# A four-layer image kernel on one Trainium2 core: the closing block of the last image, its loads, its setup and its first product are put in another order

## The chip, the cores and the metric

The kernel runs on one core of a Trainium2 chip. What is measured is the time of one execution on the device, in microseconds (us). A core has five engines that each work through their own instructions in order: PE (TensorE, matrix products; PEld is its weight load), DVE (VectorE), ACT (ScalarE), POOL (GpSimd) and SP (SyncE, which here issues the DMA transfers). They wait for each other by semaphores. PE writes only to PSUM, of which there are eight banks.

## The reference, cut to what matters

Four layers work on four images of 64 x 64 pixels with 128 channels. Layer 0 and layer 1 contain state scans over the image. The change lies where layer 1 ends for the last image and layer 2 begins. Layer 1 closes with

```python
y = ym[:, 0] + ...                         # sum of the four scan directions, 256 channels
y = _ln(y, onorm_w, onorm_b)               # over the channels
y = y * _silu(z)
x = input + y @ out_proj_w                 # 256 -> 128 channels
h2 = _ln(x, ln2_w, ln2_b)
h2 = gelu(h2 @ fc1_w + fc1_b) @ fc2_w + fc2_b   # 128 -> 512 -> 128
return x + h2
```

and layer 2 begins with `norm = _ln(tokens, ln1_w, ln1_b)` of its first image; each pixel is then joined with its nine neighbours in two small networks (`d_w1`, `r_w1`: "drive" and "resistance") that gate a weighted mean. Layer 2 needs all of the first image before it can begin, but the first image was finished by layer 1 long before the last one.

## The kernel before, in words

An image is held as 128 channels by 4,096 pixels and cut into eight chunks of 512 pixels (`NCH` = 8, `T` = 512); a chunk of 128 channels is 256 KB. The scans of both layers come first (until about 11,020 us). The last scan's result, `yd`, is 256 channels: two halves `i` = 0, 1. For every image but the last, layer 1's closing block runs as side work between the scans. For the last image nothing is left to run beside, and class `Last` does it at the beginning of `layer2`. Everything there is in the order in which it is written (`manual_schedule`), on each engine.

`layer2` first builds `Edges` (`E`). Its constructor loads the weights `w`, `rel`, `v` (L1471 to L1477) and does the setup: small products on PE with additions on DVE (`wcen`, `wnei`, `relb`, `inb`, `w2`), `obc`, `mass`, `gsp` (with one Exp and one Ln on ACT), four memsets of `near` on POOL (L1549) and two copies into `vals` on DVE (L1551).

Then `last.early()` issues the loads of the weights `wts`, and of `x` and `z` for all chunks (L1356, L1358); `z` is the gate of layer 1, already through silu. `statistics(0, range(NCH))` is layer 2's first normalization of image 0, chunk by chunk in four steps: load `xs` (L1568, two buffers), center it by a product and copy it to `norm` with ACT (L1572, L1573), square it on POOL (L1577), and form the variance by a product that ACT copies to `rstd` (L1586, L1587). `last.late()` issues the loads of `y` (L1363). `E.roots([E.rstd])` makes reciprocal roots of all the variances by two ACT instructions over 4,096 columns (L1761, L1763).

`in_turn` then runs the generators `last.first(c)`, one per chunk: in each turn one more chunk begins, and all running chunks do one stage, the oldest first. A stage ends at `yield`. The stages of `first` are:

1. product with `neg256` into bank `out0` (one buffer), L1378: minus the mean over 256 channels
2. additions to `y` on DVE (L1382, twice), squares into `tmp` on ACT (L1383) and POOL (L1384)
3. product with `ones128` into `out1` (L1388), then `over_root`: Ln and Exp on ACT into `rs`, which has two buffers (L1367, L1368)
4. scaling by `rs`, shift, and multiplication by `z`: four scalar-tensor-tensor instructions on DVE (L1393, L1394)
5. product with the output projection into a bank `mm` (two buffers) and the residual addition on DVE (L1398, L1399)
6. centering product into `cen` (L1402), square on ACT (L1404), copy on DVE (L1405)
7. variance product into `mm` (L1408) and `over_root`
8. multiplication by `rs` on DVE (L1411)

Each product of float32 is two passes of 512 columns for each half of the channels. After all chunks have gone through `first`, `second` does the two fully connected layers with Gelu (L1423, L1424, L1428, L1429) and stores, again in turn; two pieces of `project(0, range(4))` (scale `norm` by `rstd` on POOL, L1596, then products with `wnei`, L1600) go into each of its turns. The two banks `mm` are shared by the setup, the statistics, `first`, `second` and `project`.

Of the kernel before, what the change touches and what calls it, by code (L numbers as in the profile page):

```python
# [9 lines left out]
F32 = mybir.dt.float32  # L10
# [7 lines left out]
P = 128  # L18
# [3 lines left out]
T = 512  # L22
NCH = L // T
# [17 lines left out]
def chunk(c):  # L41
    return slice(c * T, (c + 1) * T)
# [185 lines left out]
class ScanWeights:  # L228
# [27 lines left out]
    def load(self):  # L256

        nct, most = self.nct, max(TILES)
        tile = self.pool.tile([P, most * ND * (H + P)], F32, name="xpdt", tag="xpdt", bufs=1)
        self.xp = tile[:, 0 : nct * ND * H].rearrange("p (t k h) -> p t k h", t=nct, k=ND)  # L260
        at = most * ND * H
        self.dtw = tile[:, at : at + ND * nct * P].rearrange("p (k c) -> p k c", k=ND)
        self.nc.sync.dma_start(out=self.xp, in_=self.d_xp)
        for i in range(HALVES):
            self.nc.sync.dma_start(out=self.dtw[i * H : (i + 1) * H], in_=self.d_dtw)
# [1068 lines left out]
class Last:  # L1334
# [14 lines left out]
            return self.psum.tile([P, 2, T], F32, name="cen", tag="cen", bufs=2)  # L1349
        return self.psum.tile([P, T], F32, name=tag, tag=tag, bufs=2 if tag == "mm" else 1)  # L1350

    def early(self):
        self.wt = self.tile("wts", 1, (P, 1280))
        self.nc.sync.dma_start(out=self.wt, in_=self.side.w1b)
        for c in range(NCH):
            self.nc.sync.dma_start(out=self.x[c], in_=self.side.x1[self.b, :, chunk(c)])  # L1356
            for i in range(2):
                self.nc.sync.dma_start(out=self.z[c][:, i, :], in_=self.side.szd[1, self.b, i][:, chunk(c)])  # L1358

    def late(self):  # L1360
        for c in range(NCH):
            for i in range(2):
                self.nc.sync.dma_start(out=self.y[c][:, i, :], in_=self.side.yd[1, self.b, i][:, chunk(c)])  # L1363

    def over_root(self, ps, scale):
        rs = self.tile("rs")
# [4 lines left out]
    def first(self, c):  # L1371

        nc, C, side = self.nc, self.C, self.side
        x, y, z = self.x[c], self.y[c], self.z[c]
        outp = self.wt[:, 0:256].rearrange("p (t c) -> p t c", t=2)
        ps = self.bank("out0")
        for i in range(2):
            nc.tensor.matmul(ps, C.neg256, y[:, i, :], start=i == 0, stop=i == 1)  # L1378
        yield
        sq = self.tile("tmp", 2, (P, 2, T))  # L1380
        for i in range(2):
            nc.vector.tensor_add(y[:, i, :], y[:, i, :], ps)  # L1382
        nc.scalar.activation(sq[:, 0, :], y[:, 0, :], AF.Square)  # L1383
        nc.gpsimd.tensor_mul(sq[:, 1, :], y[:, 1, :], y[:, 1, :])  # L1384
        yield
        ps = self.bank("out1")
        for i in range(2):
            nc.tensor.matmul(ps, C.ones128, sq[:, i, :], start=i == 0, stop=i == 1)  # L1388
        rs = self.over_root(ps, 0.5)
        yield  # L1390
        for i in range(2):
            n, w, b = y[:, i, :], side.onw[:, i : i + 1], side.onb[:, i : i + 1]
            nc.vector.scalar_tensor_tensor(n, n, w, rs, ALU.mult, ALU.mult)  # L1393
            nc.vector.scalar_tensor_tensor(n, n, b, z[:, i, :], ALU.add, ALU.mult)  # L1394
        yield
        ps = self.bank("mm")
        for i in range(2):
            nc.tensor.matmul(ps, outp[:, i, :], y[:, i, :], start=i == 0, stop=i == 1)  # L1398
        nc.vector.tensor_add(x, x, ps)  # L1399
        yield  # L1400
        ps = self.bank("cen")[:, 0, :]
        nc.tensor.matmul(ps, C.cen128, x, start=True, stop=True)  # L1402
        sq = self.tile("tmp", 2, (P, 2, T))[:, 0, :]
        nc.scalar.activation(sq, ps, AF.Square)  # L1404
        nc.vector.tensor_copy(y[:, 0, :], ps)  # L1405
        yield
        ps = self.bank("mm")
        nc.tensor.matmul(ps, C.ones128, sq, start=True, stop=True)  # L1408
        rs = self.over_root(ps, 1.0)
        yield  # L1410
        nc.vector.tensor_mul(y[:, 0, :], y[:, 0, :], rs)  # L1411
# [21 lines left out]
def in_turn(stages):  # L1433


    waiting, running = list(stages), []
    while waiting or running:
        running += waiting[:1]
        waiting = waiting[1:]
        running = [stage for stage in running if next(stage, stage) is None]  # L1440
        yield


NB = 9
# [7 lines left out]
class Edges:  # L1452
# [8 lines left out]

    def __init__(self, tc, C, es, nb, x_in, x_out, d_w, d_rel, d_v):
        self.nc, self.C, self.x_in, self.x_out = tc.nc, C, x_in, x_out
        nc = self.nc
        wp = es.enter_context(tc.tile_pool(name="l2w", bufs=1))
        self.pool = self.ahead = None
        self.psum = es.enter_context(tc.tile_pool(name="l2p", bufs=1, space=PSUM))
        self.dram = es.enter_context(tc.tile_pool(name="l2d", bufs=1, space=DRAM))

        w = wp.tile([P, d_w.shape[1]], F32, name="w")  # L1470
        nc.sync.dma_start(out=w, in_=d_w)  # L1471
        w1 = w[:, 0:768].rearrange("p (m t c) -> p m t c", m=2, t=3)
        self.vw, self.ow = w[:, 768:896], w[:, 896:1024]
        rel = wp.tile([8, 2 * P + NB], F32, name="rel")
        nc.sync.dma_start(out=rel, in_=d_rel)
        v = wp.tile([P, d_v.shape[1]], F32, name="v")
        nc.sync.dma_start(out=v, in_=d_v)  # L1477
        ln1w, ln1b, self.ln2w, self.ln2b, vb, ob = (v[:, i : i + 1] for i in range(6))
        b1, w2 = v[:, 6:8], v[:, 8:10]
        self.db2, self.rb2, gamma, self.lam, self.ebias = (v[:, i : i + 1] for i in range(10, 15))  # L1480
# [11 lines left out]
        for m in range(2):  # L1492
            ps = self.bank()
            nc.tensor.matmul(ps[:, 0:NB], rel[:, m * P : (m + 1) * P], rel[:, 2 * P :], start=True, stop=True)
            nc.vector.tensor_scalar_add(self.relb[:, m, :], ps[:, 0:NB], b1[:, m : m + 1])
            ps = self.bank()
            nc.tensor.matmul(ps[:, 0:1], self.wcen[:, m, :], ln1b, start=True, stop=True)
            nc.vector.tensor_scalar_add(self.relb[:, m, :], self.relb[:, m, :], ps[:, 0:1])
            ps = self.bank()
            nc.tensor.matmul(ps[:, 0:1], self.wnei[:, m, :], ln1b, start=True, stop=True)  # L1500
            nc.vector.tensor_copy(self.inb[:, m : m + 1], ps[:, 0:1])
            for t in range(NB):
                nc.vector.tensor_copy(self.w2[:, m, t, t : t + 1], w2[:, m : m + 1])
        ps = self.bank()
        nc.tensor.matmul(ps[:, 0:1], self.vw, ln1b, start=True, stop=True)
        nc.vector.tensor_add(self.inb[:, 2:3], ps[:, 0:1], vb)
        for m in range(2):
            nc.vector.tensor_scalar_mul(self.wcen[:, m, :], self.wcen[:, m, :], ln1w)
            nc.vector.tensor_scalar_mul(self.wnei[:, m, :], self.wnei[:, m, :], ln1w)
        nc.vector.tensor_scalar_mul(self.vw, self.vw, ln1w)  # L1510

        mean = wp.tile([P, 1], F32, name="mean")
        nc.vector.reduce_sum(mean, self.ow, axis=AX.X)
# [3 lines left out]
        nc.tensor.matmul(ps[:, 0:1], C.cen128, ob, start=True, stop=True)  # L1517
        self.obc = wp.tile([P, 1], F32, name="obc")
        nc.vector.tensor_copy(self.obc, ps[:, 0:1])


        fold = wp.tile([P, 32], F32, name="fold")
# [7 lines left out]
        for j in range(4):  # L1530
            part = slice(32 * j, 32 * j + 32)
            nc.vector.tensor_copy(self.mass[part, part], row[part].to_broadcast([32, 32]))

        self.gsp = wp.tile([P, 1], F32, name="gsp")
        zero = wp.tile([P, 1], F32, name="zero")
# [3 lines left out]
        nc.scalar.activation(self.gsp, self.gsp, AF.Ln, bias=1.0)  # L1539
        nc.vector.scalar_tensor_tensor(self.gsp, gamma, zero, self.gsp, ALU.add, ALU.max)  # L1540
        nc.vector.tensor_scalar_add(self.gsp, self.gsp, 1e-6)

# [2 lines left out]
        for tiles in self.near:  # L1547
            for t in tiles:
                nc.gpsimd.memset(t, 0.0)  # L1549
        for t in self.vals:  # L1550
            nc.vector.tensor_copy(t.rearrange("p h w -> p (h w)"), vb.to_broadcast([P, HR * PW]))  # L1551
        self.norm = [wp.tile([P, NCH, T], F32, name=f"norm{i}") for i in range(min(nb, 2))]
        self.rstd = wp.tile([P, NCH, T], F32, name="rstd")

    def bank(self):
        return self.psum.tile([P, T], F32, name="mm", tag="mm", bufs=2)
# [314 lines left out]
def layer2(tc, C, nb, x_in, x_out, d_w, d_rel, d_v, beside, side):  # L1871
    with ExitStack() as es, tc.manual_schedule():
        E = Edges(tc, C, es, nb, x_in, x_out, d_w, d_rel, d_v)

        def run(pieces):
            for piece in pieces:
                piece()

        def statistics(b, chunks):
            return staggered([E.statistics(b, c) for c in chunks]) if b < nb else []  # L1880
# [4 lines left out]
        if True:  # L1885
            with tc.tile_pool(name="last", bufs=1) as pool:
                E.pool = pool
                last = Last(tc, C, pool, E.psum, side, nb - 1, x_in)
                last.early()
                run(statistics(0, range(NCH)))  # L1890
                last.late()
                E.roots([E.rstd])
                for _ in in_turn([last.first(c) for c in range(NCH)]):
                    pass
                pieces = project(0, range(4))
                for _ in in_turn([last.second(c) for c in range(NCH)]):
                    for _ in range(2):
                        if pieces:
                            pieces.pop(0)()
                run(pieces)  # L1900
# [3 lines left out]
            out, halves, rest = None, [], []  # L1904
            for b in range(nb):
                for s in range(2):
                    if s == 0:
                        early = project(b, [4]) + [E.edge_row]
                        ahead = merged(project(b, range(5, 8)), statistics(b + 1, range(5)))
                        second = E.rstd[:, 5:8, :]  # L1910
                    else:
                        early = []
# [18 lines left out]
                    out = E.edges(b, s, at, sides, following)  # L1931
# [3 lines left out]
            pieces = E.finish(*third)  # L1935
# [519 lines left out]
```

## Time and profile before

| | us |
|---|---|
| median of 3 runs | 12947.81 (12925.22 to 12954.68) |
| the profiled execution's own time | 12949.75 |
| its span | 12948.0 |
| busy DVE / POOL / PE / ACT over the span | 11775.1 / 9661.8 / 9408.4 / 7767.4 |
| last scan output stored, first load of `w` issued | 11021.8 |
| first product of `Last.first` (L1378) | 11066.4 |
| first Gelu of `Last.second` (L1424) | 11164.0 |

The durations and instants below come from the one profiled execution. In a line of the timeline the columns are: start, time, engine, line of the code, operation, output<-input with their shapes, count, and in brackets the idle time before it and what ended that. In the chain of waits each line is a start, a duration and the work that ended last there. In the table of stretches each engine has its busy time and, in parentheses, its count of instructions; PEclk is the granted clock of TensorE as a share of full speed, and the last two columns are the busy share of the DMA engines and GB/s.

### The profile page before, as it was taken

To read this page: it belongs to the slowest core of one execution; us is meant where nothing else is said; L and a number is where in the kernel's file an instruction comes from. 1 tells how busy PE (TensorE), PEld (TensorE's weight loads), DVE (VectorE), ACT (ScalarE), POOL (GpSimd) and SP (SyncE) were. 2 spreads that over 40 slices of the span, in tenths; PEclk is the share of its full clock that TensorE was granted. 3 is DMA by queue.
4 is the path that set the end of the run, shared out by engine and by line. 5 is a ranking of instruction groups with operands and counts; after the bars stand their busy time and mean duration, and the time that the engine had idled before them with its cause. 6 is when DMAs were issued, how large, how long until landed. Compare 5 with 4: busy or idle time off the path is not lost.

```text
span 12948.0 us, 128061 instructions
## 1 busy us (share of the span) xinstructions
PE 9408.4 (73%) x40881; PEld 2751.0 (21%) x41435; DVE 11775.1 (91%) x7219; ACT 7767.4 (60%) x10392; POOL 9661.8 (75%) x3167
## 2 busy tenths in 40 slices
PE   6777777777767677677776677776777777775799
PEld 1111111111111111111111121111112121221455
DVE  8999999999999889999999999999999999498566
ACT  4666656655666546655666555555555554476576
POOL 6887888887878778887888788888888888166200
PEclk8888899889989888998889899989898888887899
DMA  6888888898888878898878987777877876255200
GB/s 180 212 223 230 218 224 218 216 227 221 211 221 210 214 199 207 220 229 213 210 219 209 227 209 200 205 200 198 218 196 200 204 197 172 66 145 132 70 21 17
DMA packets 873449, 2463.66 MB, mean 190 GB/s; under 512 B 141887, under 2 KB 163527, under 8 KB 865095
## 3 DMA queue, kind: packets, MB, share of 16 engines
q1 hardware_dynamic: 872775, 2455.44, 74.1%
q8 instruction: 330, 5.41, 0.2%
q14 instruction: 344, 2.82, 0.1%
HBM read 2035.79 MB, written 268.17 MB: 178 GB/s over the span
## 4 chain that ended last, share of the span: by engine, by line
DVE 36%; issue 18%; PE 15%; DMA 14%; POOL 8%; ACT 7%; SPq 1%; DVEq 0%; another core or an unknown queue 0%; POOLq 0%; ACTq 0%
DVE h L478 19%; DVE h L459 13%; DMA h<-dud 8%; POOL h L459 4%; PE ms L102 3%; PE da L467 2%; POOL delta L102 2%; DMA pad<-xid 1%; PE yps L559 1%; ACT s L2128 1%; ACT da L469 1%; DMA repC<-xdd 1%; DVE s L2115 1%; PE B L504 1%; POOL low L102 1%
## 5 line engine op out<-in xcount | busy, mean ns | idle before, releaser
L459 POOL TENSOR_TENSOR h<-h,repC 128x2048 f32<-128x2048 f32 x1536 | 6952.0, 4531 | 1489.0 <-ACT state L496 1194.2
L478 DVE TENSOR_TENSOR_SCAN h<-da,state,h 128x1024 f32<-128x1024 f32 x2304 | 5293.4, 2337 | 278.8 <-ACT da L469 164.9
L469 ACT ACTIVATE da<-da,av 128x1024 f32<-128x1024 f32 x3072 | 3327.6, 1087 | 2914.9 <-PE da L467 2481.5
L467 PE MATMUL da<-dp,spread 128*128 128x512 bf16 x5802 | 2002.3, 425 | 2406.7 <-DVE h L478 2368.4
L459 DVE TENSOR_TENSOR h<-h,B 128x2048 f32<-128x2048 f32 x1536 | 3474.9, 2262 | 194.1 <-issue 91.4
L559 PE MATMUL yps<-h,gather 128*32 128x512 f32 x12288 | 1876.5, 687 | 19.4 <-issue 4.8
L478 DVE TENSOR_TENSOR_SCAN h<-da,h 128x1024 f32<-128x1024 f32 x768 | 1719.4, 2278 | 68.3 <-ACT da L469 29.2
L467 PEld LDWEIGHTS <-spread 128*128 128x128 bf16 x6144 | 589.7, 102 | 4480.6 <-issue 4086.9
L565 PE MATMUL yps<-ones,nothing 128*128 128x512 bf16 x4197 | 1237.9, 405 | 38.0 <-issue 34.4
L102 ACT ACT_TABLE_LOAD x580 | 744.1, 1283 | 12.2 <-DMA x<-in_x_dram 2.2
L102 ACT CAST parts<-delta 128x1024 bf16<-128x1024 f32 x384 | 400.6, 1043 | 548.4 <-POOL delta L102 521.4
L102 POOL TENSOR_TENSOR delta<-delta,low 128x1024 f32<-128x1024 f32 x192 | 452.3, 2356 | 264.2 <-ACT low L102 213.5
L565 PEld LDWEIGHTS <-nothing 128*128 128x128 bf16 x4409 | 383.0, 101 | 1226.3 <-issue 934.1
L2159 POOL COPY wide_total<-total 128x128 f32<-128x128 f32 x128 | 37.4, 293 | 781.1 <-DVE total L2157 214.4
L102 PE MATMUL ms<-d,wts 128*128 128x512 f32 (+3 forms) x832 | 486.8, 697 | 170.4 <-POOL d L102 67.0
L102 PE MATMUL ms<-xd,xpdt 64*128 64x512 f32 x768 | 484.6, 714 | 108.6 <-ACT delta L102 26.2
L102 POOL TENSOR_TENSOR low<-delta,xc 128x1024 f32<-128x1024 f32 x192 | 502.5, 2617 | 9.1
L2128 ACT ACTIVATE s<-s,least 128x512 f32<-128x512 f32 x512 | 368.4, 720 | 231.3 <-DVE least L2115 227.7
L542 PE MATMUL yps<-y,ident 128*128 128x512 f32 x576 | 499.2, 956 | 4.6 <-issue 1.5
L1792 POOL TENSOR_TENSOR acc<-acc,part 128x1024 f32<-128x1024 f32 x120 | 301.9, 2519 | 198.4 <-DVE part L1786 198.4
L102 ACT ACTIVATE low<-ms,av 128x512 f32<-128x512 f32 x384 | 263.7, 687 | 291.1 <-PE ms L102 266.9
L102 POOL TENSOR_TENSOR parts<-delta,parts 128x1024 bf16<-128x1024 f32 x192 | 409.2, 2132 | 29.7 <-ACT parts L102 18.4
(295 smaller groups left out, 11070.9 us busy)
## 6 DMA issues: line engine op xcount, KB each, us to landing
h<-dud SPq DMA_DIRECT2D x3072, 512.0 KB
dp<-parts SPq DMA_DIRECT2D x2304, 64.0 KB
repC<-xdd SPq DMA_DIRECT2D x192, 512.0 KB
dud<-low SPq DMA_DIRECT2D x192, 512.0 KB
spread<-gd SPq DMA_DIRECT2D x72, 1024.0 KB
pad<-xid SPq DMA_DIRECT2D x176, 256.0 KB
x<-x SPq DMA_DIRECT2D x104, 256.0 KB
yd<-y SPq DMA_DIRECT2D x96, 256.0 KB
```

Of the source, the lines that this page charges most:

```text
L102: return call(*args, **kw)
L459: engine.tensor_mul(pair, pair, t.prepared[step][name].unsqueeze(1).to_broadcast([P, 2, TS]))
L467: self.nc.tensor.matmul(da[:, cols], self.C.spread[:, jj, :], dp[:, j, cols], start=True, stop=True)
L469: self.nc.scalar.activation(da, da, AF.Exp, scale=t.W.a[:, at : at + 1])
L478: nc.vector.tensor_tensor_scan(h[:, way], da[:, way], h[:, way], 0.0 if step % NSTEP == 0 else t.states[step - 1][:, u % NG : u % NG + 1], ...
L504: self.nc.tensor.matmul(rep[:, self.half(i)], t.W.pick[at, :], t.prepared[step]["xd"][at, :], start=True, stop=True)
L542: self.nc.tensor.matmul(self.like_part(yps, k), self.C.ident, self.part(t.y, k, c, b), start=True, stop=False)
L559: self.nc.tensor.matmul(out, self.C.gather[jj], rhs, start=False, stop=jj == 3)
L565: self.nc.tensor.matmul(self.live["yps"], self.C.nothing, self.C.ones16, start=False, stop=False, skip_group_check=True)
L1792: (nc.vector if alone and pair else nc.gpsimd).tensor_add(acc, acc, part)
L2115: self.nc.vector.tensor_tensor_reduce(out=self.live["s", n][:, h, :], in0=self.live["sps", n][:, h, :], in1=self.bias[case][:, h, :], scal ...
L2128: self.nc.scalar.activation(s, s, AF.Exp, scale=-1.0, bias=self.live["least", n][:, h : h + 1], accum_out=self.live["total", n][:, h : h + 1],
```

## The change

The loads of `Last` are issued chunk by chunk, `y` first, then `z`, then `x`; `wts` follows chunk 0's `z`, and the three weight loads of `Edges` follow chunk 0. The setup of `Edges` becomes a generator of twelve pieces and a rest; these pieces, the 32 pieces of the first statistics and one piece for the roots are put into the turns of `first`, four in each from the second turn on, behind the stages of that turn. With that the setup lies in turns 1 to 3 (turns counted from 0), the first two `xs` loads in turn 4, the other statistics in turns 5 to 12 and the roots in turn 12. Of `first`, stages 1 and 2 are one stage, so a chunk takes seven stages and the block fourteen turns for fifteen.

```diff
-    def early(self):
-        self.wt = self.tile("wts", 1, (P, 1280))
-        self.nc.sync.dma_start(out=self.wt, in_=self.side.w1b)
-        for c in range(NCH):
-            self.nc.sync.dma_start(out=self.x[c], in_=self.side.x1[self.b, :, chunk(c)])
-            for i in range(2):
-                self.nc.sync.dma_start(out=self.z[c][:, i, :], in_=self.side.szd[1, self.b, i][:, chunk(c)])
-
-    def late(self):
-        for c in range(NCH):
-            for i in range(2):
-                self.nc.sync.dma_start(out=self.y[c][:, i, :], in_=self.side.yd[1, self.b, i][:, chunk(c)])
+    def load(self, c):
+        nc, side, b, cols = self.nc, self.side, self.b, chunk(c)
+        for i in range(2):
+            nc.sync.dma_start(out=self.y[c][:, i, :], in_=side.yd[1, b, i][:, cols])
+        for i in range(2):
+            nc.sync.dma_start(out=self.z[c][:, i, :], in_=side.szd[1, b, i][:, cols])
+        if c == 0:
+            self.wt = self.tile("wts", 1, (P, 1280))
+            nc.sync.dma_start(out=self.wt, in_=side.w1b)
+        nc.sync.dma_start(out=self.x[c], in_=side.x1[b, :, cols])
...
             nc.tensor.matmul(ps, C.neg256, y[:, i, :], start=i == 0, stop=i == 1)
-        yield
         sq = self.tile("tmp", 2, (P, 2, T))
...
+    def load(self):
+        for to, source in zip((self.w, self.rel, self.v), self.sources):
+            self.nc.sync.dma_start(out=to, in_=source)
+
+    def setup(self):
...
             for t in range(NB):
                 nc.vector.tensor_copy(self.w2[:, m, t, t : t + 1], w2[:, m : m + 1])
+            yield
...
         for tiles in self.near:
             for t in tiles:
                 nc.gpsimd.memset(t, 0.0)
+                yield
         for t in self.vals:
             nc.vector.tensor_copy(t.rearrange("p h w -> p (h w)"), vb.to_broadcast([P, HR * PW]))
+            yield
...
-                last.early()
-                run(statistics(0, range(NCH)))
-                last.late()
-                E.roots([E.rstd])
-                for _ in in_turn([last.first(c) for c in range(NCH)]):
-                    pass
+                last.load(0)
+                E.load()
+                for c in range(1, NCH):
+                    last.load(c)
+                setup = E.setup()
+                pieces = [lambda: next(setup, None)] * 14 + statistics(0, range(NCH))
+                pieces.append(lambda: E.roots([E.rstd]))
+                for turn, _ in enumerate(in_turn([last.first(c) for c in range(NCH)])):
+                    for _ in range(4 if turn else 0):
+                        if pieces:
+                            pieces.pop(0)()
+                run(pieces)
```

The other additions of `yield` in `setup` end the pieces for `m` = 0 and 1, for `inb` with the scaling of the weights by `ln1w`, for `obc`, for `mass` and for `gsp`. The tiles `norm` and `rstd` are made in the constructor.

More of the change, by code (lines that the diff above doesn't have):

```diff
@@ L1463, in __init__ @@
         self.nc, self.C, self.x_in, self.x_out = tc.nc, C, x_in, x_out
-        nc = self.nc
         wp = es.enter_context(tc.tile_pool(name="l2w", bufs=1))
@@ L1468, in __init__ @@
         self.dram = es.enter_context(tc.tile_pool(name="l2d", bufs=1, space=DRAM))
-        w = wp.tile([P, d_w.shape[1]], F32, name="w")
-        nc.sync.dma_start(out=w, in_=d_w)
+        self.wp, self.sources = wp, (d_w, d_rel, d_v)
+        self.w = wp.tile([P, d_w.shape[1]], F32, name="w")
+        self.rel = wp.tile([8, 2 * P + NB], F32, name="rel")
+        self.v = wp.tile([P, d_v.shape[1]], F32, name="v")
+        self.norm = [wp.tile([P, NCH, T], F32, name=f"norm{i}") for i in range(min(nb, 2))]
+        self.rstd = wp.tile([P, NCH, T], F32, name="rstd")
+    def load(self):
+        for to, source in zip((self.w, self.rel, self.v), self.sources):
+            self.nc.sync.dma_start(out=to, in_=source)
+    def setup(self):
+        nc, wp, C, w, rel, v = self.nc, self.wp, self.C, self.w, self.rel, self.v
         w1 = w[:, 0:768].rearrange("p (m t c) -> p m t c", m=2, t=3)
         self.vw, self.ow = w[:, 768:896], w[:, 896:1024]
[L1474 to L1477, printed above, removed]
         ln1w, ln1b, self.ln2w, self.ln2b, vb, ob = (v[:, i : i + 1] for i in range(6))
@@ L1532, in __init__ @@
             nc.vector.tensor_copy(self.mass[part, part], row[part].to_broadcast([32, 32]))
+        yield
         self.gsp = wp.tile([P, 1], F32, name="gsp")
@@ L1541, in __init__ @@
         nc.vector.tensor_scalar_add(self.gsp, self.gsp, 1e-6)
+        yield
         self.near = [[wp.tile([P, HR, PW], F32, name=f"near{m}{s}") for s in range(2)] for m in range(2)]
@@ L1549, in __init__ @@
                 nc.gpsimd.memset(t, 0.0)
+                yield
         for t in self.vals:
             nc.vector.tensor_copy(t.rearrange("p h w -> p (h w)"), vb.to_broadcast([P, HR * PW]))
-        self.norm = [wp.tile([P, NCH, T], F32, name=f"norm{i}") for i in range(min(nb, 2))]
-        self.rstd = wp.tile([P, NCH, T], F32, name="rstd")
+            yield
     def bank(self):
@@ L1888, in layer2 @@
                 last = Last(tc, C, pool, E.psum, side, nb - 1, x_in)
-                last.early()
-                run(statistics(0, range(NCH)))
-                last.late()
-                E.roots([E.rstd])
-                for _ in in_turn([last.first(c) for c in range(NCH)]):
-                    pass
+                last.load(0)
[10 more added lines that the diff above has]
+                run(pieces)
+                assert next(setup, setup) is setup
                 pieces = project(0, range(4))
```

## The prediction

> **What bounds the kernel now.** Whole-page shares say nothing here: the change lies in one stretch of some 220 us near 11,020 us. All times below in two or three digits are microseconds after 11,000 of the trace (25.9 is 11025.9). I read the busy time by stretch first, cut at the steps of the code: loads and setup, first statistics, first chunk until the two large ACT instructions end, the pipelined turns of `first`, their drain, `second`.
>
> ```profile
> core 0: us, PE busy (x) PEld busy (x) DVE busy (x) ACT busy (x) POOL busy (x), PEclk, DMA share, GB/s
> 11021.80:11041.50 19.70, 4.19 (x16) 3.90 (x16) 10.24 (x53) 0.41 (x2) 7.72 (x4) 0.50 0.95 322
> 11041.50:11066.00 24.50, 16.85 (x32) 5.67 (x33) 0.00 (x0) 8.78 (x15) 8.31 (x8) 0.81 0.60 193
> 11066.00:11074.60 8.60, 4.28 (x10) 1.43 (x8) 2.57 (x4) 7.92 (x4) 2.08 (x2) 1.00 0.84 315
> 11074.60:11136.60 62.00, 47.84 (x91) 19.83 (x92) 30.35 (x45) 18.56 (x30) 5.77 (x5) 0.86 0.00 0
> 11136.60:11164.00 27.40, 19.32 (x32) 6.04 (x30) 19.12 (x24) 12.46 (x20) 12.14 (x8) 0.81 0.00 0
> ```
>
> Until 66.0 no chunk of the closing block has begun. Row one is transfers (95% DMA), row two a chain of statistics in which DVE does nothing. Then the chain of waits shows who ends last:
>
> ```profile
> 11036.14 5.36 DMA z<-szd
> 11041.51 5.33 DMA xs<-x
> ...
> 11067.23 3.72 ACT rstd L1761
> 11070.97 3.62 ACT rstd L1763
> 11075.16 3.80 PE out L1388 x4
> ```
>
> The xs loads sit in SP's order behind 24 loads of x and z, the y loads behind xs, and the roots (7.36 us) hold ACT while chunk 0 waits for its square. Third, the timeline of one full turn:
>
> ```profile
> 11122.82 0.69 DVE L1399 TENSOR_TENSOR x<-x,mm 128x512 f32<-128x512 f32 x1
> 11126.32 1.28 DVE L1382 TENSOR_TENSOR y<-y,out 128x512 f32<-128x512 f32 x2
> 11127.65 1.98 PE L1378 MATMUL out<-y,neg 128*128 128x512 f32 x4 [3.16 <-DVE y L1382]
> 11131.19 1.88 PE L1398 MATMUL mm<-y,wts 128*128 128x512 f32 x4
> 11133.11 0.69 DVE L1399 TENSOR_TENSOR x<-x,mm 128x512 f32<-128x512 f32 x1
> 11137.81 0.68 DVE L1411 TENSOR_TENSOR y<-y,rs 128x512 f32<-128x512 f32 x1
> 11138.58 0.69 ACT L1367 ACTIVATE rs<-mm,eps 128x512 f32<-128x512 f32 x1 [0.57 <-DVE y L1411]
> 11139.35 10.85 POOL L1596 TENSOR_TENSOR norm<-norm,rstd 128x512 f32<-128x512 f32 x7
> 11140.45 0.69 DVE L1405 COPY y<-cen 128x512 f32<-128x512 f32 x1 [1.96 <-ACT tmp L1404]
> 11141.06 0.68 DVE L1399 TENSOR_TENSOR x<-x,mm 128x512 f32<-128x512 f32 x1
> 11142.43 1.63 DVE L1394 SCALAR_TENSOR_TENSOR y<-y,v,z 128x512 f32<-128x512 f32 x1
> ```
>
> PE's first product waits 3.16 us in each turn for the additions of the chunk before (bank out0 has one buffer): a loop of 10.29 us, 122.82 to 133.11. The next turn has no such product and takes 7.95.
>
> **The change, part by part.** *Loads.* Byte count and order change, the rate does not. The first 512 KB issued at 21.79 are w today, and their waiter starts at 25.93; they become y of chunk 0, so its product can start at 25.9 instead of 66.4. Ahead of y of chunk 1 and with it lie 2.94 MB; today 1.8 MB have moved by 30.0 (222 GB/s) and 378 GB/s follow, so it lands at 33. A chunk is then 1.31 MB, 3.5 us; all 11.7 MB are in by 57. From turn 2 on no y is late. The xs loads follow; they are first used near 68, so they are hidden.
>
> *Turns 0 to 4 (fill).* Each DVE sum takes this trace's durations: additions 1.28, four scalar-tensor-tensors 2.9, residual addition 0.6, copy 0.69; POOL square 1.04.
> Turn 0: product with the clock at 0.50, 3.5 (as for the product at 115.89, 3.46), then 1.28, 1.04: 31.8.
> Turn 1: ones product of chunk 0 to 33.7, product of chunk 1 to 35.6, additions to 36.9. Then setup pieces 1 to 4, 25.93 to 32.22 today, 5.8 here: 42.7. They stand ahead of chunk 0's scaling on DVE: exposed.
> Turn 2: scaling 45.6, additions 46.9, setup pieces 5 and 6 (3.3 today) 50.2; POOL squares until 48.1, then two memsets (1.98 each) until 52.
> Turn 3: residual 50.8, scaling 53.7, additions 55.0, the two vals copies (2.56) 57.6; POOL squares to 56.2, two memsets to 60.1.
> Turn 4: copy, residual 58.9, scaling 61.7, additions 63.0.
> So the setup's 11.7 us of DVE is paid nearly in full, though transfers would have filled some of it.
>
> *Full turns.* The product no longer waits for the additions of its own turn, because the bank was freed a turn earlier: 3.16 us off. What is next late? PE's own sum, 16 passes at 0.43, is 6.9. But the two `rs` buffers tie ACT to DVE: residual +2.8 (second L1393) frees `rs`; Ln, Exp 1.4; Square 0.65; the Ln of the older chunk 0.69, Exp 0.63, Square 0.6; copy 0.7: 8.0, just the 7.95 of the row. A turn without pieces is 8.0, not 6.9.
> Statistics pieces put up to two products (0.86 each), two ACT copies (0.58) and one POOL square into a turn. PE's sum becomes 8.6; and the older chunk's product (L1408) shares the two `mm` banks, so it waits for the first piece's copy behind Square: residual +4.9 Square, +5.5 copy, L1408 to +6.6, Ln, Exp, Square to +8.6, copy, next residual +9.2. From the residual of turn 5 at 65.6 the turns give 9.2, 8.2 (one product), 9.2, 8.5 (no new chunk), 5.5 (no additions or roots of a new chunk): 106.2. Bounds for a piece turn: 8.0 (all hidden) to 11 (nothing hidden: 8.0 plus 1.72, 1.16).
>
> *Tail and roots.* From 106.2: variance 3, center 6 and variance 4 on PE with a wait for a copy, to 108.7, L1408 and L1402 to 110.4, Square 111.7, pieces, L1408 of chunk 7 to 113.2, Ln and Exp 114.7, two copies 115.9. The roots keep their 7.36, still exposed, now ahead of the first Gelu: 123.3. Table load 1.28: Gelu at 124.6, against 164.0 today. A saving of 39.4.
>
> *What is moved past.* POOL's scale products (10.85 us) ran during the drain and there doubled four DVE operations (1.63 and 1.75 for 0.75 and 0.68): with the roots late they go behind 123.3, beside `second`, where DVE has 6.0 us of work in 81. The eight POOL squares of the statistics move the other way, from a stretch without DVE work into the turns; after the square of the new chunk DVE mostly waits for ACT, so I charge nothing, bound 8 x 1.0. SP has nothing behind the xs loads until `second` stores.
> Cost of the roots' new place: PE idles 9 us before `second`, whose first products then run at half clock: 2.5 (a four-product group is 3.78 at 0.50, 1.98 at 1.00), bounds 0 and 5.
>
> Sum: 39.4 - 2.5 = 37 us. The profiled execution took 12949.75 us with a span of 12948.0; the median is 12947.8, so 2 lower: 12947.8 - 37 = 12911.
>
> The Trainium skill, SBUF — State Buffer, section "Who interferes with whom", says that a copy on DVE in its two-port mode and any GpSimd instruction exclude each other for a whole instruction; by it the second vals copy would stand behind one near memset, and the estimate would be a gain of 35. No row of before has the two together, and memsets beside small DVE operations (25.9 to 29.6) show no doubling.
>
> **Rivals.**
> *A, the sum above (gain 26 to 46: 12922 to 12902).* For it: every term is a row, and the 8.0 loop is seen in the trace.
> *B, the pieces cost much of what they hide (gain 0 to 26).* If each of turns 5 to 8 takes 11 (44 for 35.1: 9 us more), and each setup hop waits behind a product of `first` on PE's queue (about 1 us for each of 8 hops), 17 goes: gain 20, 12928. For it: in-order engines, shared `mm` banks. Against it: PE's sum of 8.6 fits.
> *C, more than the sum (gain 46 to 60).* The two half-clock stretches of today (from 115.89 for 3.3 us, from 102.61 for 6.5) do not come back, DVE's setup hops hide in the load time of turn 1, `second` starts warm: some 12 us more: gain 49, 12899.
> *D, slower: the PE clock is never granted in the turns.* It is 0.50 in row one, where PE waits. If interleaved waits kept it there, 72 us of products at full clock (`first` 54.7, statistics 13.7, setup 4) would take 145; today's PE waits in the turns, 22 (62.0 and 27.4 less 47.8 and 19.3 busy), come on top, and 8.6 of roots and table: Gelu at 25.9 + 145 + 22 + 8.6 = 201.5, 37 us slower, 12985. It decides below a mean clock of 0.67, where 72 us take the 107.5 left before 164.0. Against it: 0.86 and 0.81 in the turns today, and the waits shrink.
> *E, nothing at all:* the block is not where time is lost. Excluded by the chain of waits, which runs through it without a parallel branch.
>
> **How the numbers follow.** A 0.63, B 0.20, C 0.09, D 0.05 and other slower ways 0.03, E nil. About 0.2%, 26 us, is what a measurement can tell from no change: the three runs before spread over 29 us. Faster by over 0.2% are A and C, 0.72; within it B, 0.20; slower D and its like, 0.08. The range takes in A, most of B and the lower part of C: 12890 to 12942.
>
> **What would show it.** Right: first L1378 product near 26, a chain without xs and z transfers, product waits of 3.16 gone from the turns, 8 to 9.5 us from residual to residual in turns 5 to 8, roots between about 116 and 123 (±8), first Gelu near 125, and all later stages only shifted. Wrong: DVE idle behind setup's PE hops, turns over 11 us, a granted clock below 0.8 from 60 to 110, or scalings at 1.6 us beside POOL through the turns.

## The result, and the profile after

The changed kernel takes 12910.83 us (median of 8 runs, 12902.01 to 12926.71) against 12945.93 (8 runs, 12924.12 to 12954.68): ratio 0.9978, 95% interval 0.9969 to 0.9987, so 0.13% to 0.31% faster. The point forecast of 12911 is met, but by luck. It was 37 us off a base of 12947.8; the medians lie 35 us apart, the ratio says 28 (17 to 40 by its interval), and the traces below bear out about 26.

Two single executions can't be subtracted as wholes here. The last scan instruction of DVE ends at 11007.84 in the trace of before and at 10991.28 in that of after, 16.6 us apart, although nothing ahead of it differs in the code; over all traces of this study that instant lies between 10980 and 11022. I therefore count from that instant: 1940.2 us to the end before, 1910.9 after, 29.2 saved before rounding. It divides into 0.5 from there to the first load, 30.0 from the first load to the first Gelu of `second` (142.2 and 112.2), and -1.3 behind it.

Only the 30.0 can be taken from one pair of traces. The 0.5 is scatter: over all traces the first load comes 13.5 to 14.0 us after the scan. The -1.3 hides a larger loss. From the first Gelu to the end, the three traces with the roots still ahead of `first` (before and the experiments `join_only` and `order_only`) take 1784.0, 1780.9 and 1780.9 us, so the same code scatters by 3; the nine with the new place take 1784.4 to 1787.8. The loss is seen whole where it arises, in the first chunk of `second`. Before:

```profile
11164.02 0.69 ACT L1424 ACTIVATE y<-cen,bias 128x512 f32<-128x512 f32 x1
11164.76 1.98 PE L1423 MATMUL cen<-y,wts 128*128 128x512 f32 x4 [2.58 <-ACT y L1424]
...
11172.12 0.75 DVE L1429 SCALAR_TENSOR_TENSOR x<-mm,v,x 128x512 f32<-128x512 f32 x1 [8.69 <-PE mm L1428]
```

After (L1421 is the Gelu, L1420 its product, L1426 the residual addition):

```profile
11116.91 0.69 ACT L1421 ACTIVATE y<-cen,bias 128x512 f32<-128x512 f32 x1
11117.65 3.78 PE L1420 MATMUL cen<-y,wts 128*128 128x512 f32 x4 [9.20 <-ACT y L1421]
...
11129.04 0.75 DVE L1426 SCALAR_TENSOR_TENSOR x<-mm,v,x 128x512 f32<-128x512 f32 x1 [21.30 <-PE mm L1425]
```

From the Gelu to that addition it is 8.1 us before and 12.1 after; the granted clock over the stretch is 1.00 and 0.59. The three traces named all have 8.1 here, the nine others 11.9 to 12.3, and the eighth addition is still 4.0 us late in after. So the change saves 30.0 and pays back 4.0: about 26 us. All block times below are from the issue of the block's first load (11004.75 in after) to the first Gelu.

The same table of stretches for after, cut at 19.7 us, behind the residual addition of turn 4, at the start of the roots, at the first Gelu and 81 us on (line numbers move: L1376 is the product L1378 was, L1379 the additions, L1381 POOL's square, L1385 the ones product, L1365 the Ln into `rs`, L1390 and L1391 the scaling, L1396 the residual addition, L1399 the centering product, L1401 the square behind it, L1402 the copy, L1405 the older chunk's product, L1408 the last multiplication, L1596 the copy to `rstd`):

```profile
core 0: us, PE busy (x) PEld busy (x) DVE busy (x) ACT busy (x) POOL busy (x), PEclk, DMA share, GB/s
11004.75:11024.45 19.70, 11.41 (x24) 5.08 (x24) 5.96 (x21) 2.58 (x4) 2.19 (x2) 0.67 0.92 312
11024.45:11048.95 24.50, 20.37 (x38) 8.26 (x38) 21.38 (x51) 5.41 (x11) 8.81 (x5) 0.79 0.68 248
11048.95:11108.25 59.30, 54.63 (x119) 21.61 (x117) 37.73 (x54) 30.70 (x53) 16.88 (x14) 0.97 0.09 27
11108.25:11116.91 8.66, 0.20 (x1) 0.00 (x0) 0.00 (x0) 8.60 (x3) 1.23 (x2) 0.78 0.00 0
11116.91:11198.00 81.09, 68.68 (x140) 26.56 (x141) 5.26 (x7) 27.49 (x40) 7.35 (x7) 0.94 0.06 23
```

In the first stretch, the transfers (92% DMA) now have products of the chunks beside them; PE is busy 11.4 us for 4.2. In the third PE is busy 54.6 of 59.3 us at a clock of 0.97, where it had 0.86 and 0.81. The fourth is the price of the roots' new place: 8.7 us in which ACT works and the other engines next to nothing.

One full turn with pieces, from the timeline of after, residual addition to residual addition:

```profile
11074.74 0.68 DVE L1396 TENSOR_TENSOR x<-x,mm 128x512 f32<-128x512 f32 x1
...
11076.03 1.88 PE L1376 MATMUL out<-y,neg 128*128 128x512 f32 x4
...
11078.24 1.28 DVE L1379 TENSOR_TENSOR y<-y,out 128x512 f32<-128x512 f32 x2
...
11079.55 0.57 ACT L1596 COPY rstd<-mm 128x512 f32<-128x512 f32 x1
...
11080.17 1.13 PE L1405 MATMUL mm<-tmp,ones 128*128 128x512 f32 x2 [0.54 <-ACT rstd L1596]
...
11081.33 0.69 ACT L1365 ACTIVATE rs<-mm,eps 128x512 f32<-128x512 f32 x1 [0.73 <-PE mm L1405]
...
11083.19 0.69 DVE L1402 COPY y<-cen 128x512 f32<-128x512 f32 x1 [3.08 <-ACT tmp L1401]
...
11083.90 0.69 DVE L1396 TENSOR_TENSOR x<-x,mm 128x512 f32<-128x512 f32 x1
```

The product L1376 has no wait in brackets any more. What ends last now is the copy of a statistics piece (at 11079.55), which holds the bank that L1405 needs: the turn takes 9.16 us, as worked out (9.2).

### The profile page after: what moved, and what is told of

Same layout as the page of the kernel before. It is cut to its first block, busy times and chain, and to the rows that moved or that the text cites. A ratio compares the mean times of both kernels' runs of the same rounds, so it can differ in the third digit from the quotient of the medians.

```text
span 12902.2 us, 128082 instructions
## 1 busy us (share of the span) xinstructions
PE 9366.9 (73%) x40881; PEld 2741.6 (21%) x41435; DVE 11778.0 (91%) x7219; ACT 7769.0 (60%) x10392; POOL 9663.1 (75%) x3167
```

## The experiments

Each was judged by its block time in its own trace, because the scans ahead vary by more than most effects. Before is 142.2 us, after 112.2; `after_again`, the same kernel, has 111.9. The first residual addition comes 34.5 to 35.3 us after the first load in three traces in which nothing ahead of it differs (`after`, `after_again`, `ln_psum`), so differences below 1 us are not read. Line numbers of a run differ by a few lines from those of the kernel that it is made from.

**The join alone** (`join_only`), on the kernel before:

```diff
         for i in range(2):
             nc.tensor.matmul(ps, C.neg256, y[:, i, :], start=i == 0, stop=i == 1)
-        yield
         sq = self.tile("tmp", 2, (P, 2, T))
```

> The kernel before with the join alone: the product with neg256, its additions and squares are one stage; loads, setup, statistics and roots stand where they were. Measure: from the issue of the block's first load to the first Gelu (before 142.2 us, after 112.2), and the intervals from one residual addition to the next (before 9.4, 13.3, 11.8, 10.3, 8.0). My theory: the product no longer waits 3.16 us for the additions of the chunk before, what is left is the loop through the two rs buffers: the intervals become 8.0 each, the half-clock stretches go with the idle time, 128 us. Rival (the join is worth nothing by itself, order and pieces bring the gain): 140 to 142.

Measured: 129.1 us. The residual intervals are 6.3, 7.3, 7.9, 7.9, 8.0. From its timeline:

```profile
11117.57 0.68 DVE L1398 TENSOR_TENSOR x<-x,mm 128x512 f32<-128x512 f32 x1
...
11118.67 1.88 PE L1378 MATMUL out<-y,neg 128*128 128x512 f32 x4
...
11125.51 0.68 DVE L1398 TENSOR_TENSOR x<-x,mm 128x512 f32<-128x512 f32 x1
```

The product waits for nothing, and the turn is 7.94 us, the loop through the two `rs` buffers, not PE's 6.9. (That it is these buffers is read from the waits; no run had a third one.) The two intervals that held slow first products in before (13.3 and 11.8, with products of 3.78 and 3.46 us) shrink most, so the join takes out the wait and the slow products with it. It is worth 13.2 us by itself; the rival falls.

**The order of loads alone** (`order_only`), on the kernel before, `load(c)` as in the change but without the setup's weights:

```diff
-                last.early()
+                for c in range(NCH):
+                    last.load(c)
                 run(statistics(0, range(NCH)))
-                last.late()
                 E.roots([E.rstd])
```

> The kernel before with the new order of loads alone: y, z, x chunk by chunk; the setup, all statistics and the roots still stand ahead of the first product, and the stages are not joined. My theory: early y is worth nothing while the statistics stand ahead of it, and the xs loads now sit behind 16 more transfers, so the first product moves 11 us later: 153 us from first load to first Gelu (before 142.2). Rival (y late is what bounds the block): shorter than before, about 130.

Measured: 152.6 us. From the timeline (first load issued at 10993.8):

```profile
11028.70 3.75 PE L1570 MATMUL mm<-xs,cen 128*128 128x512 f32 x4 [24.55 <-DMA xs<-x]
...
11047.60 1.88 PE L1376 MATMUL out<-y,neg 128*128 128x512 f32 x4
```

The first centering product comes 34.9 us after the first load for 25.2 before, behind 16 more transfers. The new order by itself costs 10.4 us.

**The change without the join** (`unjoined`), the `yield` put back into after:

```diff
             nc.tensor.matmul(ps, C.neg256, y[:, i, :], start=i == 0, stop=i == 1)
+        yield
         sq = self.tile("tmp", 2, (P, 2, T))
```

> The kernel after with the yield between the first product and its additions put back. My theory: in turns with a new chunk the product waits again for the additions of the chunk before, the statistics' products behind it in PE's order move later too, and with them the copies that hold the older chunk's Ln: a turn with pieces takes 12 us for 9.2, the block 112.2 + 14 = 126 us. Rival (the pieces fill the gap, so the join no longer matters): 112 to 115.

Measured: 128.7 us, intervals up to 15.0. From its timeline:

```profile
11070.17 1.28 DVE L1380 TENSOR_TENSOR y<-y,out 128x512 f32<-128x512 f32 x2
...
11071.51 2.57 PE L1376 MATMUL out<-y,neg 128*128 128x512 f32 x4 [3.16 <-DVE y L1380]
...
11073.88 1.91 PE L1582 MATMUL mm<-xs,cen 128*128 128x512 f32 x2
...
11075.83 0.59 ACT L1583 COPY norm<-mm 128x512 f32<-128x512 f32 x1 [4.24 <-PE mm L1582]
```

The old wait of 3.16 us is back, the statistics' product stands behind it in PE's order and cannot fill it, and its copy is late in turn. The join is worth 16.6 us here.

**y late** (`late_y`): pieces and join as in after, but x and z of all chunks and the setup's weights ahead of y.

```diff
-                last.load(0)
+                last.load(0, "zx")
                 E.load()
                 for c in range(1, NCH):
-                    last.load(c)
+                    last.load(c, "zx")
+                for c in range(NCH):
+                    last.load(c, "y")
```

> The kernel after with x and z of all chunks (and the setup's weights) loaded ahead of y, as before; pieces and join as in after. My theory: y of chunk 0 lands 18 us later, nothing else can be done until then because setup and statistics stand behind the first additions, so the block is 17 us longer: 129 us. Rival (setup on DVE bounds the first turns, not the loads): 112 to 116.

Measured: 132.8 us. From its timeline (first load issued at 10993.9):

```profile
11013.02 10.49 SPq L1356 DMA_DIRECT2D y<-yd  x16
...
11018.56 3.75 PE L1378 MATMUL out<-y,neg 128*128 128x512 f32 x4 [32.23 <-DMA y<-yd]
```

The first product begins 24.6 us after the first load for 3.6, and every later residual interval is that of after within 0.02: the 20.6 us are the arrival of y. I had put the delay at 18 and the loss at 17; of the 21.0 the fill absorbs less than half a microsecond. So y first is worth 20.6 us with the pieces in the turns and the join, and less than nothing without them. The pieces need it as well: `late_y` has the join and the pieces and is 3.7 us longer than the join alone. No run has the order and the join without the pieces.

**Memsets ahead** (`memset_ahead`), on after:

```diff
         self.wp, self.sources = wp, (d_w, d_rel, d_v)
+        self.near = [[wp.tile([P, HR, PW], F32, name=f"near{m}{s}") for s in range(2)] for m in range(2)]
+        for tiles in self.near:
+            for t in tiles:
+                nc.gpsimd.memset(t, 0.0)
...
-                nc.gpsimd.memset(t, 0.0)
                 yield
```

> The kernel after with the four near memsets issued on POOL ahead of everything (in the constructor), where POOL is idle; the pieces keep their number and places. Measure: first load to first Gelu, 112.2 us in after. My theory: in after the four mass copies take 3.77 us for 0.73 and the two vals copies 3.40 for 2.56 because POOL runs a memset beside them; without that the copies are back at 0.73 and 2.56 and the block takes 107 to 108. Rival (these copies lie beside a wait for the half-clock products, which ends last anyway): 111 to 112.

Measured: 108.9 us, 3.2 less, between the two expectations and nearer to mine. From its timeline:

```profile
11065.94 0.73 DVE L1544 COPY mass<-row 32x32 f32<-32x32 f32 x4
...
11072.56 3.40 DVE L1564 COPY vals<-v 128x2244 f32<-128x2244 f32 x2
...
11072.81 1.97 POOL L1381 TENSOR_TENSOR tmp<-y 128x512 f32<-128x512 f32 x1 [7.52 <-ACT tmp L1380]
```

The `mass` copies are back at 0.73, which accounts for 3.0 of the 3.2. The `vals` copies stay at 3.40: there I was wrong, it is POOL's square that they meet, and both lose (1.97 for 1.04).

**The clock through the setup** (`warm`), on after; the added products of zeros are used by nothing:

```diff
                         if pieces:
                             pieces.pop(0)()
+                        if turn == 1:
+                            idle = E.psum.tile([P, 2, T], F32, name="cen", tag="cen", bufs=2)
+                            for i in range(2):
+                                for n in range(2):
+                                    tc.nc.tensor.matmul(idle[:, i, :], C.nothing, C.ones16, start=n == 0, stop=n == 1)
```

> The kernel after with four extra bf16 products of zeros (128 x 512, into a cen bank that is not yet used) behind each of the four setup pieces of turn 1; they compute nothing that is used. My theory: PE stays busy through the setup's hops, the clock is kept, the ones product and the first product of turn 2 take 1.9 us each for 3.76 and 3.02, and the block is 2 to 3 us shorter, 109 to 110. Rival (the clock falls whatever runs there, or the extra products cost as much as they bring): 112 to 114 with the two products still over 3 us, or at 1.9 with nothing gained.

Measured: 117.9 us, 5.8 more. From its timeline:

```profile
11025.70 1.76 PE L1913 MATMUL cen<-ones,nothing 128*128 128x512 bf16 x4
...
11027.29 1.88 PE L1385 MATMUL out<-tmp,ones 128*128 128x512 f32 x4
...
11029.01 1.88 PE L1376 MATMUL out<-y,neg 128*128 128x512 f32 x4
...
11043.73 7.21 DVE L1561 COPY vals<-v 128x2244 f32<-128x2244 f32 x2
...
11045.89 3.87 POOL L1558 MEMSET near<- 128x2244 f32 x2
```

The two products do fall to 1.88 us, as I said they would, but three of the four groups of extra products ran at half clock (1.76 to 1.87) and put the ones product 4.9 us later; the first residual addition comes 1.9 us later than in after. The rival was right: the fillers cost more than they bring. The other 3.8 us are a loss that neither expectation had: this time both memsets came in ahead of the second `vals` copy, and the two copies took 7.21.

**Setup from turn 0** (`setup_turn0`), on after:

```diff
-                last.load(0)
-                E.load()
+                last.load(0, E.load)          # called behind chunk 0's two loads of y
...
-                    for _ in range(4 if turn else 0):
+                    for _ in range(4):
```

> The kernel after with the setup's weights loaded right behind chunk 0's y and the pieces begun in turn 0 instead of turn 1 (four in each turn as before, all one turn earlier). My theory: setup pieces 1 to 4 then run while DVE waits for chunk 1's y, so some 4 to 6 us of them are hidden: 107 us (104 to 110). Rival (on PE the setup's hops now stand ahead of chunk 0's ones product and chunk 1's first product, which pays it all back; and the roots a turn earlier hold ACT ahead of chunk 7's last Ln): 112 or more.

Measured: 107.5 us, 4.7 less. From its timeline (first load issued at 11017.2):

```profile
11034.34 2.67 PE L1377 MATMUL out<-y,neg 128*128 128x512 f32 x4
...
11114.75 3.71 ACT L1771 ACTIVATE rstd<-rstd,eps 128x4096 f32<-128x4096 f32 x1
...
11122.02 0.67 ACT L1366 ACTIVATE rs<-mm,eps 128x512 f32<-128x512 f32 x1
```

The setup's hops on PE do delay chunk 1's first product (17.1 us after the first load for 12.5), but DVE has done pieces 1 to 4 by then. The number came as expected, the reason only in part. The residual addition of turn 4 comes 2.6 us earlier than in after and the last one 2.1; the other 2.6 us come behind it, because the statistics and the roots end a turn earlier. The rival's second half came too, at a small price: the roots stand ahead of chunk 7's last Ln (11122.02).

**Ln straight from PSUM** (`ln_psum`), on after:

```diff
         def variance():
-            self.variance(at["sq"], self.rstd[:, c, :])
+            if b:
+                self.variance(at["sq"], self.rstd[:, c, :])
+                return
+            ps = self.bank()
+            nc.tensor.matmul(ps, C.ones128, at["sq"], start=True, stop=True)
+            nc.scalar.activation(self.rstd[:, c, :], ps, AF.Ln, bias=C.eps)
...
-                pieces.append(lambda: E.roots([E.rstd]))
+                pieces.append(lambda: tc.nc.scalar.activation(E.rstd, E.rstd, AF.Exp, scale=-0.5))
```

> The kernel after with the Ln of image 0's roots done chunk by chunk where the variance is taken from PSUM (the ACT copy to rstd becomes an Ln with bias), so that only the Exp over 4,096 columns is left as the last piece. My theory: the roots are exposed in full, so 3.7 us go, less 0.1 per turn: 108.5. Rival (the roots lie beside chunk 7's last stages and the table load): 111 to 112.

Measured: 107.9 us, 4.3 less. The end of its ACT timeline:

```profile
11114.30 3.62 ACT L1909 ACTIVATE rstd<-rstd 128x4096 f32<-128x4096 f32 x1
11117.93 1.28 ACT L1421 ACT_TABLE_LOAD   x1
```

Behind the last residual addition 3.6 us are saved, nearly the whole Ln of 3.71 us: nothing hid it. The other 0.6 comes from an earlier start of the first turns, where this edit changes nothing.

**After once more, and the three edits together** (`after_again`, `all_three`), five rounds each beside the kernel before on one chip.

> The kernel after once more, unchanged, against the kernel before in five rounds. From the traces so far the change is worth 30 us up to the first Gelu and costs 1 us behind it: 29 us, a ratio of 0.9977. If the 35 us between the medians of the first measurement were the change's worth, the ratio would be 0.9973. The part of the program ahead of the block differs by up to 42 us between single executions, so one time alone settles nothing.

Measured: 12911.62 us (11 runs), ratio 0.9978, interval 0.9969 to 0.9988; 111.9 us in its trace and 1910.4 from the scan's end for 1910.9. A gain is confirmed; the interval (some 16 to 40 us) holds 26, 29 and 35 alike and does not choose between them.

> The kernel after with three of the edits together: near memsets ahead of everything, the setup's weights behind chunk 0's y with pieces from turn 0 on, and the Ln of image 0's roots taken from PSUM. My theory: three separate losses (the port shared by POOL and DVE, DVE's setup in front of chunk 0's scaling, exposed roots), so the gains add: 112.2 - 3.2 - 4.7 - 4.3 = 100 us from first load to first Gelu, 41 us faster than before in all, ratio 0.9968. Rival (memsets and setup are one and the same loss, since both only fill the wait for chunk 1's y): 103 to 104.

Measured: 101.4 us, 10.8 less than after where the three single gains sum to 12.2; 1899.6 us from the scan's end to the end. Behind the last residual addition the gains add in full (6.2 us); ahead of it 1.4 is missing, of which 0.6 is the earlier start of `ln_psum`. The three losses are separate but for the rest, some 0.8 us. The whole kernel takes 12905.0 us (6 runs), ratio to before 0.9969, interval 0.9957 to 0.9980. That is the fastest of the three; its interval overlaps that of after, so the lead over after rests on the trace.

## Why the prediction was right or wrong, point by point

The instants of the prediction against the trace of after, both in microseconds after the first load:

| step of the prediction | forecast | measured |
|---|---|---|
| first product | 4.1 | 3.6 |
| additions of chunk 1 end | 15.1 | 15.9 |
| setup pieces 1 to 4 end | 20.9 | 22.3 |
| additions of chunk 2 end | 25.1 | 28.5 |
| setup pieces 5 and 6 end | 28.4 | 35.4 |
| additions of chunk 4 end | 41.2 | 48.7 |
| residual addition of turn 5 | 43.8 | 51.2 |
| the next intervals | 9.2, 8.2, 9.2, 8.5, 5.5 | 10.9, 8.0, 9.2, 8.5, 6.0 |
| roots begin | 94.1 | 103.5 |
| first Gelu | 102.8 | 112.2 |
| cost of the half clock at the start of `second` | 2.5 | 4.0 |

*Loads: right.* *Wait of 3.16 removed and the 8.0 loop that takes its place: right*, seen in `join_only`; the terms written out for the loop add to 7.5, and the 0.57 us that the Ln waits for L1411, in the row shown there, make the rest. *Piece turns: right* to 0.3 where the clock was up (7.95, 9.16 and 8.51 for 8.2, 9.2 and 8.5). *Roots fully exposed: right*, seen in `ln_psum`. Case A was the one that came, at its low end: 28 us by the ratio and about 26 by the traces, not 37. That the time itself fell on 12911 is luck: the later measurement of before is 2 us lower than the one forecast from, and the medians happen to lie 35 us apart.

*Mis-sized: turns 1 to 4*, by 7.5 us, in two terms. Before:

```profile
11021.89 7.72 POOL L1549 MEMSET near<- 128x2244 f32 x4 [9.42 <-DMA yd<-y]
...
11028.08 0.63 DVE L1503 COPY w<-v 128x1 f32<-128x1 f32 x9
...
11033.36 0.73 DVE L1532 COPY mass<-row 32x32 f32<-32x32 f32 x4
...
11035.40 2.56 DVE L1551 COPY vals<-v 128x2244 f32<-128x2244 f32 x2
```

After:

```profile
11020.67 1.15 POOL L1381 TENSOR_TENSOR tmp<-y 128x512 f32<-128x512 f32 x1 [5.85 <-DVE y L1379]
11020.85 1.26 DVE L1491 TENSOR_TENSOR wnei<-w 128x256 f32<-128x256 f32 x1
...
11025.33 3.76 PE L1385 MATMUL out<-tmp,ones 128*128 128x512 f32 x4
...
11028.88 3.02 PE L1376 MATMUL out<-y,neg 128*128 128x512 f32 x4
...
11031.94 1.28 DVE L1379 TENSOR_TENSOR y<-y,out 128x512 f32<-128x512 f32 x2 [1.98 <-PE out L1376]
...
11034.39 3.88 POOL L1558 MEMSET near<- 128x2244 f32 x2
...
11035.09 3.77 DVE L1539 COPY mass<-row 32x32 f32<-32x32 f32 x4
...
11044.75 3.40 DVE L1561 COPY vals<-v 128x2244 f32<-128x2244 f32 x2
```

First, I let the clock stay up once it had come; through the small products of the setup it fell again (0.59 from 11023.0 to 11031.3), and the first two products of turn 2 took 3.76 and 3.02 us for 1.88 each: 3.0. DVE waited 1.98 us for the second of them, so no more than 2.0 of the 3.0 were on the path. That the block would be shorter by this with the clock kept is not shown, since in `warm` the fillers ate it. Turn 5 lost 1.7 over its forecast; there L1405 and L1399 ran slow as well (1.58 and 1.91 for 1.02), and in `setup_turn0`, whose turns had the clock at 1.00 throughout, no such turn takes longer than 9.2.

Second, the port that POOL and DVE share. The sum charged nothing for it, though by the prediction's own instants the memsets (48.1 to 52) lie beside setup pieces 5 and 6 (46.9 to 50.2), to which the `mass` copies belong. Four copies of 32 x 32 elements beside two memsets took 3.77 us for 0.73, and `memset_ahead` gets back 3.2. The rule that the prediction quoted from the Trainium skill (SBUF — State Buffer, "Who interferes with whom") is borne out in kind: the `vals` copies lost 0.84 us, and in `warm`, where the memsets came between, 4.65. I applied it to the large copies alone and let memsets "beside small DVE operations" pass as harmless by the stretch 25.9 to 29.6. What stood beside them there were copies of 128 x 1: nine of them took 0.63 us, as in after beside an idle POOL. So that stretch was a fair reading of those copies and none of the 32 x 32 ones; what separates the two was not tried. POOL's squares cost something too: the addition into `wnei` took 1.26 us beside one for 0.42, and three additions into `fold` 1.37 beside another for 0.65, both also in `memset_ahead`, where no memset was near.

*A term put at nothing: the statistics' squares in the turns.* Beside them two scalings and a multiplication took 1.44, 1.41 and 1.33 us for 0.75, 0.75 and 0.68. That is 2.0 us of DVE time within the bound of 8, and little of it shows: the last interval is 6.0 for 5.5.

*Mis-sized: the half clock at the start of `second`*, 4.0 us for 2.5, within its bounds of 0 and 5.

*The rivals.* C's warm clock at the start of `second` did not come: its first four products took 3.78 us. D is excluded by the clock of 0.97 in the turns. B's setup hops behind products on PE's queue are not seen in after: pieces 1 to 4 end 1.4 us late, of which 0.8 is the late start and the rest the addition into `wnei`. Of its turns of 11 us only turn 5 came (10.9), with the slow products named above.

## What to carry to other kernels

Moving loads forward pays only when the work that needs them moves forward too: the order alone cost 10.4 us, and with the pieces in place it is worth 20.6. When a wait is taken out of a pipelined turn, look for the next loop of waits (here two small buffers between ACT and DVE, 8.0 us) before counting on the engine's own sum. Side pieces need a place on every engine that they touch; a memset on an idle POOL is not free for whatever DVE does meanwhile (here 3.0 us for four small copies). Idle time that is moved to just ahead of a stretch of products is paid for in that stretch as well (4.0 us here).

## What the runs showed of the hardware that I had not expected

- Four tiny copies can be held for whole memsets: 0.73 us became 3.77, about 1.5 memsets more; nine still smaller ones (128 x 1) were not held at all.
- In these traces who came first decided: the two `vals` copies took 3.40 us in after, where the two memsets behind them took 5.05, and 7.21 in `warm`, where the memsets came in between and took 3.87.
- In every full turn looked at, the DVE copy out of bank `cen` (L1405 of before) starts only when ACT's square out of the same bank has ended (in the trace of before, a square ends at 11140.42 and the copy starts at 11140.45), though both only read it. It is part of the 8.0 loop; whether the chip or the program asks for it was not tried.
- The scans ahead of the block end up to 42 us apart in twelve executions. What varies there stays open.
